# A mixture layer and a diffusion step on one core: where token splits, sums, a weight load and the last rows are placed

## The chip, the cores and the metric

The kernel runs on one core of a Trainium2 chip. TensorE (PE in the profile) multiplies matrices, VectorE (DVE), ScalarE (ACT) and GpSimd (POOL) work elementwise, and SyncE (SP) issues most of the transfers between the chip's memory and the on-chip buffers. Matmul results land in PSUM banks; everything else lies in SBUF. Each engine works through its own instructions in order and waits, where needed, for others. The metric is the device time of one execution in microseconds, the median of several runs. A profiled execution is one more run, and its span is the time from its first to its last instruction.

## The reference

There are 128 batch entries with 64 steps of 256 features each. The first layer is a mixture of experts, the second a step of diffusion over steps and features.

```python
s0 = relu(x @ swi[0]) @ swo[0]               # two shared experts, 256 -> 1024 -> 256
s1 = relu(x @ swi[1]) @ swo[1]
eo = relu(x @ wi[type]) @ wo[type]           # one of five experts by the entry's type
w  = softmax(relu(concat(eo[:,0], s0[:,0], s1[:,0]) @ g1) @ g2)   # from step 0 alone
x  = x + eo*w[0] + s0*w[1] + s1*w[2]
# second layer: edges are reflected, in features (x) and in steps (y)
x  = x + zX*lap_x(x) + zY*lap_y(x) + zR*x*(1 - x)
```

`zX`, `zY` and `zR` are given for each batch entry. All values are 32-bit floats.

## The kernel before, in words

**Precision.** TensorE takes operands of the type fp32r, which are less exact than fp32. The kernel therefore splits each operand into a high part (a ScalarE copy that rounds, called "hi") and a low part (source less hi, on VectorE or GpSimd, "lo"), and forms hi*hi + hi*lo + lo*hi: three matmuls for one product. `split` (L116) writes both parts.

**Seven products.** The first matmul of each expert, on a 2 x 2 grid of blocks, is done with seven block products in place of eight. This needs sums of blocks: `sum_wi` for the weights (S1 to S4), `sum_x` (L194) for the tokens (T1 to T4; T2 needs T1, T4 needs T2). The tokens B11, B21, B22 and T1 to T4 are then split by `split_x` (L207). `unit` (L627) does the seven products: pa with B11 and then B21, pb with T2, T3 and T4 on top of a copy of pa, pd with T1 and then B22. It makes from them four hidden blocks, the h rows of the profile, with the help of u and c. The first two units of the kernel are formed without this scheme (`plain_units`, L676).

**Items.** An item is one expert on two token tiles (of four steps each) and has four units (q = 0 to 3), one for each quarter of the 1024 hidden values. The second matmul (the acc rows) follows one unit behind, in rows i = 0 to 3 of 128 tokens for each of the two tiles: "wide" matmuls over 512 columns take the hi part of the hidden values with both parts of the weights, "narrow" ones over 256 columns take the lo part. `tile_a` and `tile_b` (L738 on) list them, `evacuate` (L747) takes a finished row out of PSUM. The order of the items:

- items 0 and 1: the shared experts on the first two tiles; their rows are kept in memory (sh_d);
- items 100 to 104 (`EI` and on): a typed expert on sixteen batch entries each, gathered by type (`load_fours`, L403), rows stored to memory (eo_d); some 42 us each, from 90 to 304 us;
- groups (`stream`): the typed experts for the batch entries that are left, to 448 us. `store_group` (L920) stores each group's rows. Behind it stand two regions under a condition on the number of slots (`tc.If`, L1100), for batch entries that may not fit; every engine passes their branches;
- items 2 to 15: the shared experts on the other tiles, an even and an odd item for each pair of tiles, some 41.5 us each. Their evacuation adds the row, weighted by the gate, into yb on VectorE. The gate is computed in item 2 (`gate_shared` to `gate_weights`; gis, pt_s and pgs in the profile); diffusion of a finished tile (`diffuse_a` and `diffuse_b`, in two halves; la, lb, lq in the profile) runs in the items behind.

**Order.** Nothing is left to a scheduler in these items: instructions stay on each engine in the order in which the code issues them. Side work is hung at slots k of the item: `at(k, ...)` is the hook behind step k % 4 of unit k // 4, slots 16 and 17 come at the item's end, among the matmuls of its last rows, and slot 17 is behind the last row matmuls that are ahead of the next item. So slots 15 to 17 hold what the next item needs: for expert items `next_fours` places four sums and seven splits of its tokens, for the odd shared items `next_x` (L1117). In `stream` and in the If regions the order is left to the scheduler. SP issues loads and stores in the code's order, and one that waits holds those behind it; the store of the last group goes over GpSimd's queue instead.

**The end.** The last item's last unit is `end_unit` (L824). It forms its hidden values without the seven products, finishes the rows of the first of its two tiles and then those of the second, does diffusion of the last rows between them on VectorE, and takes the last but one step's diffusion on TensorE: fp32 matmuls with diagonal matrices (`diagonals`, the diag and lin rows). The very last step has a neighbour on one side only and goes over VectorE (end_a, end_q).

Every matmul has L88 in the profile (`mm`), every operation of VectorE, ScalarE and GpSimd L103 (`keep`), most loads and stores L114 (`dma`), every branch L1101.

Of the kernel before, what the change touches and what calls it, by code (L numbers as in the profile page):

```python
# [16 lines left out]
P = 128  # L17
# [14 lines left out]
ST = 4  # L32
# [13 lines left out]
def cond_resid_kernel(ctx: ExitStack, tc: tile.TileContext, xg, xs, xn, itok, z, we, ws, g1, g2, out):  # L46
# [356 lines left out]
    def load_fours(n):  # L403

        s0 = (n - EI) * 4 * NB
        gval[n] = expert_of(s0)
        xr = [opool.tile([P, ST + 2, D], F32, tag="yb", name=f"xr{n}_{l}") for l in range(2)]
        xr = [t.rearrange("p r d -> p (r d)")[:, 0 : 4 * S * NB].rearrange("p (j c) -> p j c", c=2 * S) for t in xr]
        load_batches(s0, 4 * NB, lambda j: xr[j // (2 * NB)][:, j % (2 * NB), :])
        for k in range(2):  # L410
            for l in range(2):
                xraw[n, k, l] = xr[l][:, :, k * S : (k + 1) * S]
# [263 lines left out]
    def plain_units():  # L676
# [17 lines left out]
        for i in (T1, T2):  # L694
            sum_x(0, i, vec)
        run(tile(0, 1))
        split_wo(0)
        keep_wo(0)
        sum_wi(2, gps)
# [117 lines left out]
    def diagonals():  # L817

        d = slot2("diag")
        last_op["d"] = [d[:, i * P : (i + 1) * P] for i in range(3)]  # L820
        for dst, f in zip(last_op["d"], (zt[:, 0:1], zt[:, 1:2], cz[:, 0:1])):
            act.activation(dst, ident, AF.Copy, scale=f)

    def end_unit(n, gaps, hooks):  # L824
# [10 lines left out]
        wide, narrow = tile_a(n, q)  # L835
        run(wide)
        run(narrow)
        diffuse_a(t - 1, 0, vec, act)
        run(plain_tile(n, q, 1, w, (last_op["x"], xop[p, B22]), psum, True))
        for i in range(2):  # L840
            run(row_work(n, 1, i, range(NF - 2), True))
        for step in range(3):
            diffuse_b(t - 1, 0, step)
        diffuse_a(t - 1, 1, vec, act)
        halo(t)
        for i in range(2):
            run(row_work(n, 1, i, (NF - 2, NF - 1), True))
            run(row_work(n, 1, i, range(NF), False))
            if i == 0:
                for step in range(3):  # L850
                    diffuse_b(t - 1, 1, step)
        diffuse_a(t, 0, vec, act)
        for step in range(3):
            diffuse_b(t, 0, step)
        for i in range(2, ST):
            if i == ST - 1:
                diffuse_a(t, 1, vec, act)
                for step in range(3):
                    diffuse_b(t, 1, step)
            run(row_work(n, 1, i, range(NF), True))  # L860
            run(row_work(n, 1, i, range(NF), False))

        r = ST
        dx, dy, dc = last_op["d"]
        lin = psum("lin")[:, 0:D]
        mm(lin, dc, y[:, r, :], True, False)
        mm(lin[:, 1:D], dx, y[:, r, 0 : D - 1], False, False)
        mm(lin[:, 0 : D - 1], dx, y[:, r, 1:D], False, False)
        mm(lin[:, 0 : D : D - 1], dx, y[:, r, 1 : D - 1 : D - 3], False, False)
        mm(lin, dy, y[:, r - 1, :], False, False)  # L870
        mm(lin, dy, y[:, r + 1, :], False, True)
        sq, a, q = (small.tile([P, D], F32, tag="s2", name=f"end_{k}") for k in "saq")
        c = y[:, r + 1, :]
        vec.tensor_tensor(a[:, 1 : D - 1], c[:, 0 : D - 2], c[:, 2:D], ALU.add)
        act.activation(q, c, AF.Identity, bias=cz[:, 0:1], scale=cz[:, 1:2])
        edges(a, c, act)
        vec.tensor_mul(q, q, c)
        vec.scalar_tensor_tensor(q, a, zt[:, 0:1], q, ALU.mult, ALU.add)
        vec.scalar_tensor_tensor(q, y[:, r, :], cz[:, 2:3], q, ALU.mult, ALU.add)
        nc.scalar.dma_start(out[:, S - 1, :], q)  # L880
        vec.scalar_tensor_tensor(sq, y[:, r, :], cz[:, 1:2], y[:, r, :], ALU.mult, ALU.mult)
        vec.tensor_tensor(sq, lin, sq, ALU.add)
        nc.sync.dma_start(out[:, S - 2, :], sq)
# [36 lines left out]
    def store_group(g, i):  # L920
        acc = gacc[g][i]
        o = small.tile([P, D], F32, tag="s2", name=f"ge{g}_{i}")
        if g < NRUN - 1:
            act.activation(o, acc[:, 0, :], AF.Copy)
            vec.tensor_add(o, acc[:, 1, :], o)
        else:
            both = small.tile([P, 2, D], F32, tag="s2", name=f"gb{g}_{i}")
            act.activation(both, acc, AF.Copy)
            gps.tensor_add(o, both[:, 0, :], both[:, 1, :])
# [84 lines left out]
    def load_unit(u):  # L1014
        if u < 2 * NQ:
            load_ws(u)
        else:
            load_we(*divmod(u, NQ))
# [42 lines left out]
    def next_fours(n, sums, splits):  # L1061
# [15 lines left out]
        next_fours(EI, (8, 10, 14, 15), (15, 16, 16, 16, 17, 17, 17)),  # L1077
# [4 lines left out]
    for n in range(EI, EI + NQUAD):  # L1082
        parts = [weights_of(n)]
        if n + 1 < EI + NQUAD:
            parts += [
                at(0, lambda: load_fours(n + 1)),
                next_fours(n + 1, (6, 10, 14, 15), (15, 16, 16, 16, 17, 17, 17)),
# [29 lines left out]
    def next_x(p):  # L1117
        if p == NP:
            return {}
        s = {i: [lambda i=i: sum_x(p, i, gps)] for i in (T1, T2, T3, T4)}  # L1120
        x = {i: [lambda i=i: split_x(p, i, gps if i in (B11, B21, B22) else vec)] for i in range(7)}
        return {
            (1, 0): [lambda: load_x(p)],
            (2, 0): s[T1] + s[T2],
            (2, 1): s[T3],
            (2, 2): s[T4] + x[B11],
            (2, 3): x[T2] + x[B21],
            (3, 0): x[T3],
            (3, 1): x[T1],
            (3, 2): x[T4],  # L1130
            (3, 3): x[B22],
        }
# [27 lines left out]
    for p in range(1, NP):  # L1160
        ta, tb = 2 * p, 2 * p + 1
        for e in range(2):
# [19 lines left out]
            elif n == 3:  # L1182
# [3 lines left out]
                parts.append(diffusion(0, 7, True, 7, (0, 1, 1)))  # L1186
# [65 lines left out]
```

## Time and profile before

| | us |
|---|---|
| runs | 1051.44, 1051.68 (median), 1052.11 |
| profiled execution | 1050.79 |
| its span | 1049.1 |
| TensorE busy | 1036.2 |
| VectorE busy | 803.1 |
| ScalarE busy | 570.5 |
| GpSimd busy | 199.5 |

The granted TensorE clock was 0.998 of full speed on the mean. In the timeline a row gives the start, the duration, the engine, the line, the operation, the output and input tiles (without their numbers) and sizes, how many of the same kind follow one another ("x3"), and in square brackets the idle time just before it with what ended it. PEld is TensorE's loading of weights, beside the matmuls. The end of a matmul is modelled, so starts are surer than durations. An engine's name with a q is its own issue of instructions, of a transfer or a branch.

### The profile page before, as it was taken

What the parts mean: (1) busy time and instruction counts of PE and PEld (TensorE: products, weight loads), DVE (VectorE), ACT (ScalarE), POOL (GpSimd) and SP (SyncE); (2) the same over time, 40 slices, a digit from 0 to 9 for tenths busy, and PEclk for the clock granted to TensorE, in tenths of its full rate; (3) what the DMA queues carried; (4) which work ended last, traced back from release to release, by engine and by line L of the source; (5) the groups of instructions that cost most, each with busy time, mean ns of one, the idle gap of its engine ahead of it and who ended that gap; (6) DMA issues with size and microseconds to landing.
All of it is one profiled execution on the core that took longest, in us unless ns stands there. A gap on an engine that the chain in (4) does not pass through costs nothing.

```text
span 1049.1 us, 15713 instructions
## 1 busy us (share of the span) xinstructions
PE 1036.2 (99%) x5433; PEld 882.3 (84%) x5433; DVE 803.1 (77%) x1462; ACT 570.5 (54%) x1081; POOL 199.5 (19%) x199
## 2 busy tenths in 40 slices
PE   9999999999999999999999999999999999999997
PEld 6878888888888889978788888888888888888887
DVE  7887987978777657747979768768687687687777
ACT  6566666766655546643644645446345354364362
POOL 2000000000013001221422521322242242052020
PEclk9999999999999999999999999999999999999999
DMA  6486232331456956555435325334344253254321
GB/s 216 184 286 205 82 103 91 101 121 51 131 178 227 334 175 209 184 180 218 155 127 176 135 107 201 121 121 166 110 166 163 68 209 128 76 175 160 108 76 46
DMA packets 67282, 159.14 MB, mean 152 GB/s; under 512 B 7712, under 2 KB 34848, under 8 KB 67200
## 3 DMA queue, kind: packets, MB, share of 16 engines
q1 hardware_dynamic: 64576, 149.19, 41.1%
q0 software_dynamic: 2480, 8.78, 2.3%
q8 instruction: 44, 0.72, 0.3%
q14 instruction: 38, 0.31, 0.1%
q10 hardware_dynamic: 144, 0.13, 0.0%
HBM read 126.88 MB, written 31.20 MB: 151 GB/s over the span
## 4 chain that ended last, share of the span: by engine, by line
PE 51%; DVE 4%; issue 1%; ACT 1%; DVEq 0%; ACTq 0%
PE acc L88 27%; PE pb L88 10%; PE pd L88 7%; PE pa L88 6%; DVE lq L103 2%; PE pu L88 1%; DVE h_5b L103 0%; DVE pd L103 0%; DVE c L103 0%; PE pgs L88 0%; DVE h_5a L103 0%; ACT u L103 0%; DVE yb L103 0%; DVE la L103 0%; DVE end_q L103 0%
## 5 line engine op out<-in xcount | busy, mean ns | idle before, releaser
L88 PE MATMUL pb<-x,wi 128*128 128x512 f32 x729 | 209.1, 395 | 1.5 <-ACT u L103 1.1
L88 PEld LDWEIGHTS pb<-x,wi 128*128 128x128 f32 x729 | 129.5, 189 | 29.9 <-ACT u L103 5.2
L103 ACT ACTIVATE u<-pb 128x512 f32<-128x512 f32 x162 | 96.8, 597 | 104.3 <-PE pb L88 98.2
L88 PE MATMUL pd<-x,wi 128*128 128x512 f32 x486 | 138.2, 393 | 2.0 <-DVE c L103 1.5
L88 PE MATMUL pa<-x,wi 128*128 128x512 f32 x486 | 137.1, 390 | 0.7 <-PEq L1101 0.7
L103 ACT ACTIVATE pb<-pa 128x512 f32<-128x512 f32 x81 | 47.2, 583 | 129.9 <-PE pa L88 129.9
L103 DVE SCALAR_TENSOR_TENSOR yb<-acc,wgt,yb 128x256 f32<-128x256 f32 x216 | 99.4, 482 | 22.8 <-PE acc L88 19.1
L88 PEld LDWEIGHTS pd<-x,wi 128*128 128x128 f32 x486 | 90.7, 188 | 24.6 <-DVE c L103 4.0
L88 PEld LDWEIGHTS pa<-x,wi 128*128 128x128 f32 x486 | 89.9, 188 | 18.9 <-issue 0.9
L103 DVE TENSOR_TENSOR c<-pd,u 128x512 f32<-128x512 f32 x81 | 55.8, 689 | 38.6 <-ACT u L103 18.6
L103 POOL TENSOR_TENSOR la<-yb 128x508 f32<-128x508 f32 (+1 forms) x28 | 31.7, 1132 | 281.6 <-ACT yb L103 280.0
L103 POOL TENSOR_TENSOR x<-xr,x 128x512 fp32r<-128x512 f32 x23 | 30.8, 1341 | 237.4 <-ACT x L103 156.2
L88 PE MATMUL up<-gxh,gw 128*128 128x256 f32 (+1 forms) x288 | 74.0, 331 | 0.0
L88 PE MATMUL gacc<-gw,gh 128*128 128x512 f32 (+1 forms) x288 | 62.7, 360 | 0.0
L103 ACT ACTIVATE gh<-up 128x256 fp32r<-128x256 f32 (+1 forms) x72 | 34.2, 477 | 42.4 <-PE up L88 41.4
L88 PEld LDWEIGHTS gacc<-gw,gh 128*128 128x128 f32 x288 | 49.9, 188 | 8.4
L88 PE MATMUL acc<-wo,h_1b 128*128 128x256 f32 (+1 forms) x172 | 56.7, 333 | 0.0
L88 PE MATMUL acc<-wo,h_6b 128*128 128x256 f32 (+1 forms) x172 | 56.7, 334 | 0.0
L88 PE MATMUL acc<-wo,h_7b 128*128 128x256 f32 (+1 forms) x172 | 56.7, 333 | 0.0
L88 PE MATMUL acc<-wo,h_2b 128*128 128x256 f32 (+1 forms) x172 | 56.6, 333 | 0.0
L88 PE MATMUL acc<-wo,h_0b 128*128 128x256 f32 (+1 forms) x172 | 56.6, 333 | 0.0
L88 PE MATMUL acc<-wo,h_3b 128*128 128x256 f32 (+1 forms) x172 | 56.6, 333 | 0.0
(253 smaller groups left out, 2536.6 us busy)
## 6 DMA issues: line engine op xcount, KB each, us to landing
wi<-wi_d SPq DMA_DIRECT2D x55, 896.0 KB, 4.5
gwr<-we_in SPq DMA_DIRECT2D x32, 512.0 KB, 5.3
wsr<-we_in SPq DMA_DIRECT2D x20, 512.0 KB, 5.5
xr<-xs_in SPq DMA_DIRECT2D x32, 256.0 KB, 5.6
yb<-xn_in SPq DMA_DIRECT2D x16, 512.0 KB, 5.8
y_out<-lq SPq DMA_DIRECT2D x30, 256.0 KB, 2.1
wi_d<-wi SPq DMA_DIRECT2D x8, 896.0 KB, 4.1
xr<-xg_in SPq DMA_DIRECT2D x80, 64.0 KB, 1.9
```

Source lines behind the costliest of these rows:

```text
L88: nc.tensor.matmul(out_ap, lhsT=lhsT, rhs=rhs, start=start, stop=stop, skip_group_check=True)
L103: ins = call(*args, **kwargs)
```

## The change

- `plain_units`: the split of the first output weights (`split_wo(0)`, with its store) goes ahead of two token sums, T1 and T2, on VectorE.
- `load_fours`: for the first expert item the first weights are asked for ahead of the sixteen gathered loads of tokens; `load_unit` leaves them out later.
- Sums and splits: the first expert item's first two sums move from slots 8 and 10 to 10 and 12. For all expert items the split of T1 moves from slot 17 to 16.
- `store_group`: the last group is evacuated like the others, a ScalarE copy of one half and a VectorE add, in place of a copy of both halves and a GpSimd add.
- `next_x`: for the tokens of items 6 and on, sums go from GpSimd to VectorE at slots 10, 12, 14 and 15, and splits go to slots 15 to 17, with GpSimd left with that of B22 alone. For those of item 4 (made in item 3) GpSimd keeps them, with the splits placed later.
- `diffusion` in item 3: its second half comes three slots sooner.
- `end_unit`: the rows of the first tile are done one by one; diffusion goes ahead of the last hidden values; the last step goes over TensorE as well, with a diagonal of 2 zY, and so the matrices are those of zX, zY and 2 zY.

```diff
@@ load_fours
+        if n == EI:
+            load_we(n, 0)
@@ plain_units
-        for i in (T1, T2):
-            sum_x(0, i, vec)
         run(tile(0, 1))
         split_wo(0)
         keep_wo(0)
+        for i in (T1, T2):
+            sum_x(0, i, vec)
@@ diagonals
-        for dst, f in zip(last_op["d"], (zt[:, 0:1], zt[:, 1:2], cz[:, 0:1])):
+        for dst, f in zip(last_op["d"], (zt[:, 0:1], zt[:, 1:2], cz[:, 2:3])):
@@ end_unit
-        wide, narrow = tile_a(n, q)
-        run(wide)
-        run(narrow)
+        for i in range(ST):
+            for wide in (True, False):
+                run(row_work(n, 0, i, (2 * q, 2 * q + 1), wide))
         diffuse_a(t - 1, 0, vec, act)
-        run(plain_tile(n, q, 1, w, (last_op["x"], xop[p, B22]), psum, True))
+        out_b = plain_tile(n, q, 1, w, (last_op["x"], xop[p, B22]), psum, True)
+        for step in range(3):
+            diffuse_b(t - 1, 0, step)
+        run(out_b)
         for i in range(2):
             run(row_work(n, 1, i, range(NF - 2), True))
-        for step in range(3):
-            diffuse_b(t - 1, 0, step)
         diffuse_a(t - 1, 1, vec, act)
         halo(t)
+        for step in range(3):
+            diffuse_b(t - 1, 1, step)
...
-        mm(lin, dc, y[:, r, :], True, False)
-        mm(lin[:, 1:D], dx, y[:, r, 0 : D - 1], False, False)
-        mm(lin[:, 0 : D - 1], dx, y[:, r, 1:D], False, False)
-        mm(lin[:, 0 : D : D - 1], dx, y[:, r, 1 : D - 1 : D - 3], False, False)
-        mm(lin, dy, y[:, r - 1, :], False, False)
-        mm(lin, dy, y[:, r + 1, :], False, True)
...
+        def beside(dst, row, stop=False):
+            mm(dst[:, 1:D], dx, row[:, 0 : D - 1], False, False)
+            mm(dst[:, 0 : D - 1], dx, row[:, 1:D], False, False)
+            mm(dst[:, 0 : D : D - 1], dx, row[:, 1 : D - 1 : D - 3], False, stop)
+
+        act.activation(qb, b, AF.Identity, bias=cz[:, 0:1], scale=cz[:, 1:2])
+        diffuse_a(t, 1, vec, act)
+        vec.tensor_mul(qb, qb, b)
+        run(row_work(n, 1, 3, range(NF), True))
+        run(row_work(n, 1, 3, range(NF), False))
+        mm(lb, dy, y[:, ST - 1, :], True, False)
+        mm(lc, dyy, b, True, False)
+        beside(lc, c, True)
+        beside(lb, b)
+        mm(lb, dy, c, False, True)
+        act.activation(qc, c, AF.Identity, bias=cz[:, 0:1], scale=cz[:, 1:2])
+        for step in range(2):
+            diffuse_b(t, 1, step)
+        vec.tensor_mul(qc, qc, c)
+        diffuse_b(t, 1, 2)
+        vec.tensor_tensor(qc, lc, qc, ALU.add)
+        nc.scalar.dma_start(out[:, S - 1, :], qc)
+        vec.tensor_tensor(qb, lb, qb, ALU.add)
+        nc.sync.dma_start(out[:, S - 2, :], qb)
@@ store_group
-        if g < NRUN - 1:
-            act.activation(o, acc[:, 0, :], AF.Copy)
-            vec.tensor_add(o, acc[:, 1, :], o)
-        else:
-            both = small.tile([P, 2, D], F32, tag="s2", name=f"gb{g}_{i}")
-            act.activation(both, acc, AF.Copy)
-            gps.tensor_add(o, both[:, 0, :], both[:, 1, :])
+        act.activation(o, acc[:, 0, :], AF.Copy)
+        vec.tensor_add(o, acc[:, 1, :], o)
@@ load_unit
+        if u in wsr:
+            return
@@ items 1 and 100 to 104
-        next_fours(EI, (8, 10, 14, 15), (15, 16, 16, 16, 17, 17, 17)),
+        next_fours(EI, (10, 12, 14, 15), (15, 16, 16, 16, 16, 17, 17)),
...
-                next_fours(n + 1, (6, 10, 14, 15), (15, 16, 16, 16, 17, 17, 17)),
+                next_fours(n + 1, (6, 10, 14, 15), (15, 16, 16, 16, 16, 17, 17)),
@@ next_x
-        s = {i: [lambda i=i: sum_x(p, i, gps)] for i in (T1, T2, T3, T4)}
-        x = {i: [lambda i=i: split_x(p, i, gps if i in (B11, B21, B22) else vec)] for i in range(7)}
...
+        if p == 2:
+            sums, splits, eng, slow = (8, 9, 10, 11), (12, 15, 14, 16, 16, 17, 16), gps, (B11, B21, B22)
+        else:
+            sums, splits, eng, slow = (10, 12, 14, 15), (15, 16, 16, 16, 16, 17, 17), vec, (B22,)
+        return join(
+            at(4, lambda: load_x(p)),
+            *(at(k, lambda i=i: sum_x(p, i, eng)) for i, k in zip((T1, T2, T3, T4), sums)),
+            *(
+                at(k, lambda i=i: split_x(p, i, gps if i in slow else vec))
+                for i, k in zip((B11, T2, B21, T3, T1, T4, B22), splits)
+            ),
+        )
@@ item 3
-                parts.append(diffusion(0, 7, True, 7, (0, 1, 1)))
+                parts.append(diffusion(0, 7, True, 4))
```

## The prediction

> **What bounds the kernel now.** I read the page's engine row first, then the waits of TensorE, then TensorE's timeline around each wait.
>
> ```profile
> PE 1036.2 (99%) x5433; PEld 882.3 (84%) x5433; DVE 803.1 (77%) x1462; ACT 570.5 (54%) x1081; POOL 199.5 (19%) x199
> ```
>
> TensorE is busy for nearly the whole span, VectorE for three quarters, GpSimd for a fifth. So only two things shorten the run: a wait of TensorE, and the stretch behind its last matmul. The waits of TensorE (what it waited for: total us, times, longest):
>
> ```profile
> PE pd L88 <- DVE c L103: 1.5, 1, 1.5
> PE pb L88 <- ACT u L103: 1.1, 4, 0.5
> PE pgs L88 <- DVE gis L103: 1.0, 1, 1.0
> ```
>
> These understate a stall, since the end of a matmul is modelled. In the timeline, 512-column matmuls start every 0.228 us when nothing is late (256-column ones every 0.118), and after a stall the next one takes 0.11 more. So I measure each stall as the distance of two starts less that rate, and add 0.11. An expert boundary shows it:
>
> ```profile
> 132.19 0.39 PE L88 MATMUL acc<-wo,h_7b 128*128 128x512 f32 x1
> 132.64 0.73 PE L88 MATMUL pb<-x,wi 128*128 128x512 f32 x2
> ```
>
> 0.45 between two starts, less 0.228, plus 0.11: 0.33 us, with no wait shown at all. Everything below is in these units. The span is 1049.1 us, its execution 1050.79, the runs' median 1051.68: the median lies 0.9 above the profiled execution, and I carry that over.
>
> **The change part by part.**
>
> *Start (plain units).* TensorE's first row matmul comes at 14.06 instead of 13.42 (0.65 with the 0.11), waiting for the VectorE split wo of 13.32 to 14.00. VectorE had made two sums at 10.80 and 11.52 before it. With the sums behind it, wo is done at about 13.3, before TensorE asks at 13.5. But the two sums (0.60 + 0.72) then push later VectorE work; a gap of 0.42 at 21.3 takes part of it, and c of the first full unit, at about 26.2, would meet a TensorE that arrives 0.65 sooner, at 25.95. That gives back 0.4. Value 0.25; ends 0 and 0.65.
>
> *First expert weights and sums (load_fours, slots 10 and 12).* The dearest stall, on VectorE and then on TensorE:
>
> ```profile
> 68.05 0.69 DVE L103 TENSOR_TENSOR xt<-xr,xr 128x512 f32<-128x512 f32 x1 [2.48 <-DMA xr<-xg_in]
> ...
> 69.26 0.68 DVE L103 TENSOR_TENSOR wi<-wsum,wi 128x512 fp32r<-128x512 f32 x1
> 69.86 0.69 DVE L103 TENSOR_TENSOR c<-pd,u 128x512 f32<-128x512 f32 x1
> ...
> 70.60 0.98 PE L88 MATMUL pd<-x,wi 128*128 128x512 f32 x3 [1.50 <-DVE c L103]
> ```
>
> The sum waits 2.48 us for the gathered tokens, and c, for which TensorE waits, stands behind it. TensorE's start at 68.24 needed three matmuls (0.69), so 68.93 against 70.60: 1.66 + 0.11 = 1.77. Two slots later the sum is behind c; c's inputs are there at about 67. The weights, too, came late: SP asks for 16 token rows first, then for the weights.
>
> ```profile
> 56.65 9.60 SPq L114 DMA_DIRECT2D xr<-xg_in  x16
> 68.05 0.34 SPq L114 DMA_DIRECT2D wsr<-we_in  x1
> 75.67 0.98 PE L88 MATMUL pb<-x,wi 128*128 128x512 f32 x3 [0.20 <-ACT u L103]
> ```
>
> They landed at 74.41; ScalarE's split of them stood in front of u, and TensorE stalled 0.36 + 0.11. Asked for ahead of the rows they land near 62. The price: SP issues a table read and that transfer first, about 0.75 us, so the last token row lands near 68.8 instead of 68.03. Behind the waiting sum on VectorE now stand h_5b, h_5a and the pd add of that unit; their first reader on TensorE is the narrow rows at about 75, so some 5 us of cover hide it. SP's stores behind the rows move by 0.75, then regain it, as the later weight load is gone from there. Value 2.2; ends 1.8 and 2.3.
>
> *T1's split from slot 17 to 16.* At each of five expert boundaries (90, 132, 174, 216, 258 us) pb, a ScalarE copy, waits behind three copies of x, which wait behind the second eo copy:
>
> ```profile
> 130.44 1.14 ACT L103 ACTIVATE x<-xt 128x512 fp32r<-128x512 f32 x2
> ...
> 132.00 0.59 ACT L103 ACTIVATE pb<-pa 128x512 f32<-128x512 f32 x1
> ```
>
> One of the three, 0.52 us, moves ahead of the eo copies, where ScalarE waits on TensorE anyway; each stall is 0.2 without its 0.11. All five go: 0.27 + 4 x 0.325 = 1.57. Value 1.55; ends 1.2 and 1.6.
>
> *Last group's add.* GpSimd leaves it, so gis no longer waits for GpSimd's branches:
>
> ```profile
> 448.78 0.73 POOL L103 TENSOR_TENSOR ge<-gb 128x256 f32<-128x256 f32 x1 [9.07 <-ACT gb L103]
> 452.53 0.69 DVE L103 COPY gis<-pt_s 128x512 f32<-128x512 f32 x1 [6.15 <-POOLq L1101]
> 453.27 2.05 PE L88 MATMUL pgs<-gis,g1t 128*128 128x128 f32 x16 [0.98 <-DVE gis L103]
> ```
>
> That stall is 1.15. But VectorE itself now adds first and then passes the two branches, and the next item's pa waits for VectorE to be past them. Half copies (0.38, as an eo copy) end near 448.5 and 448.75, the adds (0.41) at 448.9 and 449.3; VectorE's table read and two branches took 1.18 before (445.97 to 447.15). That gives 450.1 to 450.5 for pa, which started at 449.03: a new wait of 1.1 in place of 1.15. Behind VectorE there stands only gis. The store of the group comes some 0.6 sooner, which nobody waits for. Value 0; ends -0.4 and +0.5.
>
> *Item 3 (diffusion earlier, sums off GpSimd's way).* Stalls at 520.48 (0.70 + 0.11), 521.97 (0.41 + 0.11) and three small ones: 1.65. They come where diffusion's second half meets GpSimd's sums. Three slots (2.5 us each) earlier that half is out of the way, but must fit among the gate's row additions. Value 1.0; ends 0.4 and 1.65.
>
> *Items 5 to 13, odd ones: four sums and two splits from GpSimd to VectorE.* This is the part to weigh. While GpSimd works, VectorE is slow:
>
> ```profile
> 601.26 1.66 DVE L103 SCALAR_TENSOR_TENSOR h_5b<-c,h_5b 128x512 fp32r<-128x512 f32 x1 [0.70 <-ACT h_5b L103]
> 602.84 0.68 DVE L103 SCALAR_TENSOR_TENSOR h_5a<-pb,h_5a 128x512 fp32r<-128x512 f32 x1
> ```
>
> h_5b takes 1.66, its twin 0.68. In item 5 four such rows are longer by 0.57, 0.43, 0.44 and 0.97: 2.4 us lost to GpSimd. The Trainium skill (SBUF — State Buffer, "Who interferes with whom") says that VectorE with two SBUF inputs and GpSimd share one port pair as an exclusive lock, and that the second to issue fully blocks. By the rule the six operations, 1.30 each, may cost VectorE 7.8, and taking them over (6 x 0.60 = 3.6) would free 4.2 us; by the row they cost 2.4, and VectorE has 1.2 us more to do per odd item. I take the row: VectorE goes from 32.87 busy in 42 us to about 34.1. Stalls to be won: item 5 0.45, 7 0.44, 11 0.52, 13 0.28: 1.67.
>
> Against that, VectorE's order at the end of the item. With t = 0 at the next item's first matmul, TensorE wants T2 after pa (0.7) and eight wide rows (1.8), at 2.5; B21 at 3.2, T3 at 5.7, T1 at 6.4, T4 at 9.0, B22 at 9.7. The item's first four rows end by t = -4.2 (ten wide and sixteen narrow matmuls follow: 2.3 + 1.9); their eight evacuations of 0.48, the first at -4.8 as row 0 ends sooner, keep VectorE until about -1.1; then T2 at -0.5, B21 0.1, T3 0.7, T1 1.3; four more evacuations to 3.2, T4 3.8. Smallest slack 3.0 us. ScalarE has no evacuations here, so pb isn't late. I leave 0.1 per boundary for what I can't see: value 1.2; ends -1.5 (a 0.6 us stall at each of five) and +1.7.
>
> *Tail.* The last row's matmuls end here, and everything behind is exposed:
>
> ```profile
> 1042.36 0.48 DVE L103 SCALAR_TENSOR_TENSOR yb<-acc,wgt,yb 128x256 f32<-128x256 f32 x1
> 1042.89 0.70 PE L88 MATMUL lin<-yb,diag 128*128 128x256 f32 x2 [0.29 <-DVE yb L103]
> 1045.53 0.42 DVE L103 TENSOR_TENSOR end_s<-lin,end_s 128x256 f32<-128x256 f32 x1
> 1045.99 0.33 SPq L883 DMA_DIRECT2D y_out<-end_s  x1
> ```
>
> The row's last matmul starts at 1039.96, but VectorE, continuous since 1025.66, takes its result only at 1042.36. Diffusion now goes ahead of the hidden layer's last part and the rows of the first tile end one by one, so VectorE catches up and reads the row at about 1040.3, done 1040.8. Then nine fp32 matmuls in place of six, two passes of 0.215 each: those that need the last row (three for lc, four for lb) run 1041.2 to 1044.1. Of the VectorE chain behind the row (six operations, 3.1 us) only two adds are left: qb at 1044.5, the store at 1044.55 against 1045.99. Value 1.4; ends 0.9 (VectorE not caught up) and 2.0.
>
> Sum: 0.25 + 2.2 + 1.55 + 0 + 1.0 + 1.2 + 1.4 = 7.6. Profiled execution 1050.8 - 7.6 = 1043.2; median 1051.7 - 7.6 = 1044.1. All ends together: -0.4 + 0 + 1.8 + 1.2 + 0.4 - 1.5 + 0.9 = 2.4 and 10.4 (1049.3 and 1041.3).
>
> **The rivals.**
>
> *The last group's new wait is longer than the old.* VectorE's branches are passed after the adds, and both TensorE's pa and the gate hang on it. For: 1.18 us is measured with VectorE already waiting there. Against: ScalarE and TensorE passed theirs meanwhile, so only VectorE's own path counts. With 1.5 us more than I put: 1045.6, between 1045 and 1047.
>
> *VectorE gives back what GpSimd frees.* Splits move from slots 10 to 15 into 15 to 17, all in the stretch where it also evacuates. At 0.6 us per odd boundary: 1.2 + 1.5 = 2.7 less gain, 1046.8 (1046 to 1049). For: 1.2 us more work; B22, still on GpSimd, can hold the lock against an evacuation. Against: 3 us of slack, and that expert items already work in this order with only ScalarE's stall.
>
> *Slower.* The same place with a large price: VectorE reaches T2 over 3.0 us after my placement, and every us beyond it stalls TensorE at each of five boundaries. It decides at a lateness of 3.0 + (7.6 - 1.2 + 2.1) / 5 = 4.7 us: then 1054. That takes five of the eight evacuations at the contended 1.66 - 0.68 = 1 us more, with a single GpSimd split there to contend with.
>
> *The tail and item 3 give all.* 2.0 + 1.65 and the start's 0.65: 1.7 more, 1042.4; with the last group's 0.5, 1041.9.
>
> **How the numbers follow.** Likeliest (each part within its ends, 1042 to 1046): 0.62. Longer branch wait 0.12, VectorE gives back 0.15, more than my sum (below 1042) 0.05, slower 0.04, no difference 0.02. A measurement of this kernel tells 0.2%, 2.1 us, from nothing. Faster: 0.62 + 0.12 + 0.15 + 0.05 = 0.94. Predicted 1044.1; the range 1041.8 to 1047.3 leaves out the slow half of the give-back, the two last cases and what is below 1041.8.
>
> **What would show it.** Starts of TensorE: no gap at 13.4, 68.9 and 75.3; no gap at the five boundaries; a wait before item 2's first matmul of 2 us in place of 0.9, and none before pgs; h_5b in odd items at 0.7; the last yb row done before 1041 less the 6 us gained ahead. I am wrong if gaps of 0.3 or more stand at the boundaries behind items 5, 7, 9, 11 and 13, if VectorE is still continuous at the last row, or if pa of item 2 starts over 3 us after the group's last matmul.

## The result, and the profile after

Six runs of each kernel: before, 1052.11 us in the median (1051.44 to 1053.70); changed, 1043.73 us (1042.41 to 1046.41). The ratio is 0.9919, with a 95% interval of 0.9903 to 0.9935: 8.4 us less. Forecast was 1044.1, a gain of 7.6. The profiled execution of the changed kernel took 1042.87 us, with a span of 1040.7.

The page's engine row of the changed kernel, and under it the waits of TensorE (what it waited for: total us, times, longest):

```profile
PE 1031.7 (99%) x5439; PEld 884.7 (85%) x5439; DVE 810.3 (78%) x1492; ACT 572.5 (55%) x1081; POOL 154.4 (15%) x167
...
PE pa L88 <- DVEq L1104: 1.7, 1, 1.7
...
PE pb L88 <- ACT pb L103: 0.5, 2, 0.3
PE pd L88 <- DVE c L103: 0.4, 1, 0.4
```

GpSimd lost 45 us of work and VectorE gained 7. Of the three waits of before that hung on c, u and gis, two are gone from the list and one is small; a new one stands at the top, pa waiting for VectorE's sequencer.

The 8.4 us by stretches of TensorE's timeline, each from one fixed matmul to another, so that every stall in between is counted, shown or not:

| stretch | before | after | gain | forecast |
|---|---|---|---|---|
| span's start to the wide rows behind pm_cnt (start) | 39.32 | 39.40 | -0.1 | 0.25 |
| from there to the middle of item 100 (first expert weights and sums, first boundary) | 63.29 | 61.27 | 2.0 | 2.5 |
| to the middle of item 104 (four boundaries) | 167.79 | 166.25 | 1.5 | 1.25 |
| to the last group's last matmul | 177.62 | 177.61 | 0 | 0 |
| to a matmul in item 2's first unit (last group's add) | 8.30 | 8.10 | 0.2 | 0 |
| to a matmul ahead of item 3's stalls | 54.63 | 54.61 | 0 | 0 |
| to pd in item 4 (items 3 and 4) | 48.38 | 47.24 | 1.1 | 1.0 |
| to the last row's last matmul (items 5 to 15) | 480.63 | 478.53 | 2.1 | 1.2 |
| from there to the span's end (tail) | 9.13 | 7.65 | 1.5 | 1.4 |

The forecast column splits T1's 1.55 into 0.3 for the first boundary and 1.25 for the others. It adds up to 7.6; the gains add up to 8.4, the difference of the spans.

Where the sum waited for tokens before, the changed kernel has c ahead of it (SyncE's loads of the token rows, then VectorE's and ScalarE's timeline):

```profile
57.65 10.23 SPq L114 DMA_DIRECT2D xr<-xg_in  x16
...
67.64 0.69 DVE L103 TENSOR_TENSOR c<-pd,u 128x512 f32<-128x512 f32 x1 [0.19 <-PE pd L88]
68.24 0.68 DVE L103 TENSOR_TENSOR wo<-wsr,wo 128x512 fp32r<-128x512 f32 x1
69.68 0.69 DVE L103 TENSOR_TENSOR xt<-xr,xr 128x512 f32<-128x512 f32 x1 [0.75 <-DMA xr<-xg_in]
...
71.49 0.69 DVE L103 TENSOR_TENSOR pd<-pd,u 128x512 f32<-128x512 f32 x1
...
72.21 0.60 ACT L103 ACTIVATE h_4b<-pd 128x512 fp32r<-128x512 f32 x1 [1.04 <-DVE pd L103]
72.70 0.61 ACT L103 ACTIVATE wi<-wsr 128x256 fp32r<-128x256 f32 x2
73.21 0.59 ACT L103 ACTIVATE u<-pb 128x512 f32<-128x512 f32 x1
```

The stall of 1.77 is gone. But the sum still waits, now for 0.75, as the last token row landed at 69.60, and this wait reaches TensorE: the pd add (the row pd<-pd,u) stands behind the sum, ScalarE's h_4b waits for the pd add, and u, for which TensorE waits, stands behind h_4b and the weights' split (wi). TensorE's matmuls start at 73.33 and 73.86, 0.52 apart where 0.23 is due: with the 0.11 behind it 0.40 is left, where 0.47 stood before.

An expert boundary, TensorE's timeline at the place of the one shown of before:

```profile
130.25 0.39 PE L88 MATMUL acc<-wo,h_7b 128*128 128x512 f32 x1
130.47 0.84 PE L88 MATMUL pb<-x,wi 128*128 128x512 f32 x3
```

0.22 between the starts in place of 0.45. The last group (TensorE, VectorE):

```profile
445.03 0.76 DVE L103 TENSOR_TENSOR ge<-gacc,ge 128x256 f32<-128x256 f32 x2 [2.14 <-ACT ge L103]
...
446.55 0.98 PE L88 MATMUL pa<-x,wi 128*128 128x512 f32 x3 [1.74 <-DVEq L1104]
...
448.07 0.69 DVE L103 COPY gis<-pt_s 128x512 f32<-128x512 f32 x1 [2.28 <-PE pt_s L490]
...
449.69 1.95 PE L88 MATMUL pgs<-gis,g1t 128*128 128x128 f32 x16
```

pa starts 2.02 us after the group's last matmul (1.01 before), and pgs starts without a wait. The tail:

```profile
1033.01 0.28 PE L88 MATMUL acc<-wo,h_7b 128*128 128x256 f32 x1
...
1033.33 0.48 DVE L103 SCALAR_TENSOR_TENSOR yb<-acc,wgt,yb 128x256 f32<-128x256 f32 x1
...
1036.80 0.42 DVE L103 TENSOR_TENSOR end_qb<-lin_b,end_qb 128x256 f32<-128x256 f32 x1 [0.99 <-PE lin_b L88]
...
1037.25 0.33 SPq L889 DMA_DIRECT2D y_out<-end_qb  x1
```

VectorE takes the last row 0.32 us after its last matmul starts (2.40 before). From yb's start to the store it is 3.92 us (3.63 before), most of it now TensorE's work.

### The profile page after: what moved, and what is told of

Same layout as the page of the kernel before. It is cut to its first block, busy times and chain, and to the rows that moved or that the text cites. A ratio compares the mean times of both kernels' runs of the same rounds, so it can differ in the third digit from the quotient of the medians.

```text
span 1040.7 us, 15721 instructions
## 1 busy us (share of the span) xinstructions
PE 1031.7 (99%) x5439; PEld 884.7 (85%) x5439; DVE 810.3 (78%) x1492; ACT 572.5 (55%) x1081; POOL 154.4 (15%) x167
## 4 chain that ended last, share of the span: by engine, by line
PE 56%; DVE 1%; issue 0%; ACT 0%; DVEq 0%; ACTq 0%
PE acc L88 30%; PE pb L88 11%; PE pa L88 7%; PE pd L88 7%; PE pu L88 1%; DVE lq L103 0%; PE lin_b L88 0%; PE pgs L88 0%; PE lin_c L88 0%; PE pge L88 0%; DVE h_3a L103 0%; DVE c L103 0%; ACT u L103 0%; DVE pd L103 0%; DVE h_2b L103 0%
## 5 line engine op out<-in xcount | busy, mean ns | idle before, releaser
L88 PE MATMUL acc<-wo,h_4b 128*128 128x256 f32 (+1 forms) x172 | 56.5, 332 | 0.0
```

What stands on the lines that cost most here:

```text
L88: nc.tensor.matmul(out_ap, lhsT=lhsT, rhs=rhs, start=start, stop=stop, skip_group_check=True)
```

## The experiments

All kernels below are the changed one with the edit shown. Executions of one kernel lie up to 5 us apart (1042.41 to 1046.41 of the changed one, 1044.52 to 1049.60 of the first one below). Profiles of the same code differ in the first 10 us, in the two stalls at 73 and 82 us, in one stall of item 4 and, as will be seen, behind the last group. So the stretches of the profile decide, each read from a single profile, and the medians are given beside them.

### First expert weights: behind the token rows again

```diff
-        if n == EI:
-            load_we(n, 0)
```

> The changed kernel, with the first expert weights asked for where they were before, behind the sixteen token rows; the sums stay at their new slots. Of the two stalls near 70 us the first (1.77) should stay away, as it hung on the sum's slot alone. The second was 0.47 before and is still 0.40 in the changed kernel, where the weights are early: there ScalarE's h_4b waits for VectorE's pd add, which stands behind the sum that waits for tokens. If the weights' landing was a second cause behind it, the stall grows to 1 us or more here, since the split of the weights waits for them at about 74.5 while TensorE asks at 73.5. If h_4b alone makes it, it stays at 0.4 or, with the tokens 0.75 us earlier, goes to nothing.

1045.72 us in the median. The first stall stayed away; the second grew from 0.40 to 1.74. ScalarE's and TensorE's timeline:

```profile
74.50 0.61 ACT L103 ACTIVATE wi<-wsr 128x256 fp32r<-128x256 f32 x2 [2.07 <-DMA wsr<-we_in]
75.02 0.58 ACT L103 ACTIVATE u<-pb 128x512 f32<-128x512 f32 x1
...
75.65 0.73 PE L88 MATMUL pb<-x,wi 128*128 128x512 f32 x2 [1.47 <-ACT u L103]
```

So the early weights are needed. Moving the sum alone removes 1.77 at the first place and, since TensorE then arrives sooner, has 1.3 of it fall due at the second, where the weights are late. No run moved the weights alone; that c would then still wait behind the sum is argued from the profile before. From pm_cnt to the first group's first matmul the kernel takes 1.85 us more than the changed one.

### T1's split at slot 17 again

```diff
-(15, 16, 16, 16, 16, 17, 17)
+(15, 16, 16, 16, 17, 17, 17)      # in both calls of next_fours
```

> The changed kernel, with the split of T1 of the expert items back at slot 17. My theory: each of the five boundaries gets its stall of 0.27 to 0.33 us back, 1.5 us in all in the profile, and nothing else moves. Rival: the boundaries gained for another reason (GpSimd, or work that is earlier for the edits ahead of them), and stay without a stall.

One execution, 1044.76 us. All five stalls came back, 0.27 at the first boundary and 0.32 to 0.33 at the others. TensorE's timeline at the second:

```profile
131.14 0.39 PE L88 MATMUL acc<-wo,h_7b 128*128 128x512 f32 x1
131.59 0.73 PE L88 MATMUL pb<-x,wi 128*128 128x512 f32 x2
```

0.45 again. The sum of the five is 1.55. The stretch that holds the last four grew by 1.47, a little more than their starts show (1.28).

### Items 5 to 13: the engine and the place apart

The edit moves work to VectorE and moves it later. Two kernels undo one of the two.

```diff
 # the old engine at the new slots
-(10, 12, 14, 15), (15, 16, 16, 16, 16, 17, 17), vec, (B22,)
+(10, 12, 14, 15), (15, 16, 16, 16, 16, 17, 17), gps, (B11, B21, B22)
```

> The changed kernel, with the four sums and the splits of B11 and B21 of items 6 and on given back to GpSimd, at the new, late slots. If the work on VectorE is what removed the stalls of items 5, 7, 11 and 13 (GpSimd slowing VectorE), they come back in other places of the odd items, with VectorE rows of 1.0 to 1.8 us beside GpSimd's: 1.5 to 3 us over the changed kernel. If it is the later placement alone, no stall over 0.2 us stands in items 5 to 13 and the time is that of the changed kernel within 0.5 us.

```diff
 # the new engine at the old slots
-(10, 12, 14, 15), (15, 16, 16, 16, 16, 17, 17), vec, (B22,)
+(8, 8, 9, 10), (10, 11, 11, 12, 13, 14, 15), vec, (B22,)
```

> The changed kernel, with the sums and splits of items 6 and on kept on VectorE but at the slots of before (8 to 15). If GpSimd's slowing of VectorE made the stalls, they stay away: the changed kernel's time within 0.5 us. If the placement matters, VectorE's added 3.6 us now stand in the middle of the item, among c and the hidden blocks and beside the diffusion of the tile before, and the stalls of ScalarE's u and VectorE's c return at 0.3 us or more in each odd item: 1.5 to 2.5 us longer.

Medians: 1046.00 and 1046.69 us. From the gate's last matmuls in item 2 to the last row's last matmul, which holds items 3 to 15:

| | slots of before | new slots |
|---|---|---|
| GpSimd | 2.1 longer | 565.73: 2.3 longer |
| VectorE | 567.27: 3.8 longer | 563.43 |

The times are in us, and "longer" is against the changed kernel, lower right. The upper left figure is worked out from the kernel before, less the 1.1 that items 3 and 4 gained. Neither half of the edit gains anything alone; one costs a little, the other 1.7. VectorE's timeline in item 5, first of the kernel with GpSimd at the new slots:

```profile
592.77 1.19 DVE L103 SCALAR_TENSOR_TENSOR lq<-la,zt,lq 128x512 f32<-128x512 f32 x1
593.88 0.68 DVE L103 SCALAR_TENSOR_TENSOR h_4a<-pa,h_4a 128x512 fp32r<-128x512 f32 x1
594.49 1.45 DVE L103 SCALAR_TENSOR_TENSOR lq<-lb,zt,lq 128x512 f32<-128x512 f32 x1
595.86 0.68 DVE L103 TENSOR_TENSOR c<-pd,u 128x512 f32<-128x512 f32 x1
```

The diffusion rows lq take 1.19 and 1.45 while GpSimd makes its sums, and c, behind them, holds TensorE for 0.56 + 0.11, here and in two of the other four odd items. Then of the kernel with VectorE at the old slots:

```profile
596.57 0.68 DVE L103 TENSOR_TENSOR xt<-xr,xr 128x512 f32<-128x512 f32 x1
597.17 0.69 DVE L103 TENSOR_TENSOR c<-pd,u 128x512 f32<-128x512 f32 x1
597.77 0.68 DVE L103 TENSOR_TENSOR xt<-xr,xt 128x512 f32<-128x512 f32 x1
598.37 0.68 DVE L103 TENSOR_TENSOR x<-xr,x 128x512 fp32r<-128x512 f32 x1
```

Every row has its 0.68, but three sums stand ahead of c and two more rows right behind: c waits for its turn, 0.44 + 0.11 at TensorE, and once more 0.11, in each of the five odd items. In the changed kernel:

```profile
593.70 0.74 DVE L103 SCALAR_TENSOR_TENSOR lq<-lb,zt,lq 128x512 f32<-128x512 f32 x1
594.57 0.69 DVE L103 TENSOR_TENSOR c<-pd,u 128x512 f32<-128x512 f32 x1
595.18 0.68 DVE L103 TENSOR_TENSOR xt<-xr,xr 128x512 f32<-128x512 f32 x1
```

Short rows, and the sum behind c. The expectation for the first kernel was right in kind; that for the second, that a free port alone keeps the stalls away, fell.

### Item 3: diffusion's second half late again

```diff
-parts.append(diffusion(0, 7, True, 4))
+parts.append(diffusion(0, 7, True, 7, (0, 1, 1)))
```

> The changed kernel, with the second half of the diffusion in item 3 back at its old slots (seven later); the new slots of GpSimd's sums and splits in item 3 stay. The changed kernel lost 0.4 us to stalls in item 3, the one before 1.7. If diffusion's place is what mattered, a stall of u or h_4b near 518 us comes back with 0.7 to 1.3 us. If GpSimd's sums, which now start one slot apart, mattered, item 3 stays within 0.2 us of the changed kernel.

1043.17 us. The stall of u came back:

```profile
517.01 0.39 PE L88 MATMUL acc<-wo,h_5a 128*128 128x512 f32 x1
517.92 0.96 PE L88 MATMUL pb<-x,wi 128*128 128x512 f32 x3 [0.53 <-ACT u L103]
```

0.91 apart: 0.69 + 0.11. Up to item 4's stall the kernel is 0.67 longer. Items 3 to 15 are only 0.38 longer, though: item 4's stall of c, 0.65 in the changed kernel, is 0.30 here. It looks as if item 4 gave back what item 3 gains, but that isn't shown: of the nine other profiles with the changed code in items 3 and 4, five have 0.65 there and four 0.37 or 0.38, and what makes the difference is open. Item 3 itself was 1.43 longer before the change, so diffusion's place is worth about half of that. For the other 0.76 GpSimd's new slots in item 3 are left, which no run tried alone.

### Start: the two sums ahead again

```diff
+        for i in (T1, T2):
+            sum_x(0, i, vec)
         run(tile(0, 1))
         split_wo(0)
         keep_wo(0)
-        for i in (T1, T2):
-            sum_x(0, i, vec)
```

> The changed kernel, with the two token sums back ahead of the split of the first output weights. In the changed kernel the wait for wo is gone, but pb of the first full unit waits 0.5 us for the bank that VectorE's h_2b frees, behind the same two sums; from the first row matmul's place to the pm_cnt matmul both kernels take the same time. My theory: VectorE sets the pace in the first 21 us, and the order of its work only moves the wait; the wait for wo returns with 0.65, that of pb goes, and the time is that of the changed kernel within 0.3 us. Rival: the edit gained its 0.25 us and hid it behind a later landing of the first loads; then this kernel shows the wait for wo and a wait of pb, and is longer by 0.25 to 0.65.

1042.97 us. The wait for wo came back (0.55) and that of pb at 21 us (0.52) went. From the last matmul ahead of the wait for wo to pm_cnt it takes 25.55 us here, 25.60 in the changed kernel and 25.66 before. The edit moved the wait, and no gain shows: in eight other profiles that start like the changed kernel this stretch takes 25.17 to 25.82.

### Tail: the last step on VectorE again

```diff
-        lb, lc = (psum(f"lin_{k}")[:, 0:D] for k in "bc")
...
-        vec.tensor_tensor(qc, lc, qc, ALU.add)
...
+        vec.scalar_tensor_tensor(q, a, zt[:, 0:1], q, ALU.mult, ALU.add)
+        vec.scalar_tensor_tensor(q, y[:, r, :], cz[:, 2:3], q, ALU.mult, ALU.add)
```

> The changed kernel, with the very last step back on VectorE (as before the change, six fp32 matmuls with a diagonal of cz), while the order ahead of it (rows one by one, diffusion sooner) stays. In the changed kernel 7.7 us lie between the start of the last row matmul and the end of the span, in the one before 9.1. My theory: most of the 1.45 us gained comes from the order, since VectorE takes the last row 0.3 us after its last matmul and not 2.4; the matrices for the last step only move work from VectorE (3.6 us from the row to the store before) to TensorE (3.9 us). But with three more diffusion operations back ahead of the row (1.3 us) VectorE is about 1 us late for it. So 8.2 to 8.8 us here, 0.5 to 1.1 more than the changed kernel. Rival: the order alone gains all, and this kernel ends in 7.7 us or less; or it gains nothing, and the distance is 9.1 again.

1043.86 us. The tail takes 8.44 us: 0.8 more than in the changed kernel, 0.7 less than before. (In the other profiles with the changed tail it takes 7.34 to 7.80.) VectorE's timeline:

```profile
1034.06 0.48 DVE L103 SCALAR_TENSOR_TENSOR lq<-lb,zt,lq 128x256 f32<-128x256 f32 x1
1034.46 0.48 DVE L103 SCALAR_TENSOR_TENSOR yb<-acc,wgt,yb 128x256 f32<-128x256 f32 x1
1034.97 0.42 DVE L103 TENSOR_TENSOR end_a<-yb 128x254 f32<-128x254 f32 x1
...
1037.64 0.42 DVE L103 TENSOR_TENSOR end_s<-lin,end_s 128x256 f32<-128x256 f32 x1
```

The row is taken 1.4 us after its last matmul starts (1033.06), between 0.32 and 2.40. The new order and the new place of the last step gain about half each. The second gains not by a shorter way from row to store, but by the three lq rows that no longer have to come ahead of the row.

### Last group: who frees what

Three kernels. The first, with ScalarE copying both halves and VectorE adding from SBUF:

```diff
-        act.activation(o, acc[:, 0, :], AF.Copy)
-        vec.tensor_add(o, acc[:, 1, :], o)
+        act.activation(both, acc, AF.Copy)
+        vec.tensor_add(o, both[:, 0, :], both[:, 1, :])      # last group alone
```

> The changed kernel, with one thing altered: the last group's accumulators are copied out whole by ScalarE (both halves, as before the change), and VectorE adds the two halves from SBUF. My theory: item 2's first matmul waited 1.9 us in the changed kernel because the PSUM bank that it takes is freed by VectorE's add, behind which lie VectorE's branches. With ScalarE freeing the bank, the distance from the group's last matmul to pa falls from 2.02 to about 1.0 us, gis still doesn't wait for GpSimd, and pgs follows without a stall: 1.0 us less than the changed kernel, about 1042.7. Rival: TensorE waits for VectorE's branch for the sake of the order of the regions, not of the bank; then pa stays at 2.0 us and nothing changes.

1045.53 us. TensorE's timeline:

```profile
449.26 0.50 PE L88 MATMUL pa<-x,wi 128*128 128x512 f32 x1 [2.17 <-DVEq L1109]
```

pa came 2.45 us after the group's last matmul, not 1.0: the bank isn't what it waits for. VectorE's adds came later by the longer copies, and its branches with them. pa starts 0.29 us behind the start of VectorE's second branch in both kernels (446.26 and 446.55 in the changed one, 448.97 and 449.26 here). My theory fell, and the rival held in kind.

The second is the kernel with four edits, of which the first bears on this place:

```diff
+                    for k in range(2):      # last group: both halves into one
+                        mm(gacc[g][i][:, 0, :], h[j][0][:, i * P : (i + 1) * P], w[j][:, k, 256:512], ...)
...
-        vec.tensor_add(o, acc[:, 1, :], o)
...
-next_fours(EI, (10, 12, 14, 15)
+next_fours(EI, (11, 12, 14, 15)
...
-        for i in (T3, T4):
-            sum_x(0, i, vec)
         run(tile(1, 1, seeded))
+        for i in (T3, T4):
+            sum_x(0, i, vec)
...
-diffusion(2, 6)
+diffusion(2, 7)
```

> The changed kernel with four small edits, each at its own place. (1) Last group: TensorE adds both halves itself (two matmuls of 256 columns into one half in place of one of 512), so that ScalarE's copy is all that is left and neither VectorE nor GpSimd has an add; pa should come 1.0 us after the group's last matmul in place of 2.0, with no wait ahead of pgs and no stretch at half clock behind it. (2) First expert's T1 sum at slot 11 in place of 10, behind the pd add: h_4b isn't held any more, and the stalls at 73.3 (0.40) and 82 (0.38) should go. (3) The sums T3 and T4 of the first tile behind the hidden block h_3b: pb's bank is free 1.4 us sooner, and its stall of 0.5 goes. (4) Item 4's diffusion of tile 2 one slot later: c is no longer behind three long rows, and the stall of 0.65 at 554 goes. Together 1.0 + 0.7 + 0.5 + 0.6 = 2.8 us less than the changed kernel. If TensorE waits for something else at any of the places, that term is missing.

1045.91 us; none of the four terms gained. (1) VectorE passed its branches ahead of time, yet pa waited 1.89 us for TensorE's own (PEq): its second branch took 1.38 us in place of the 0.22 that it takes in every other profile here. The trace doesn't tell why. (2) The stall at 73 went, but the one at 82 grew from 0.38 to 1.01: VectorE waited 0.59 for the next weights, and T4's sum and B11's split stood ahead of h_6b. (3) pb's stall grew from 0.52 to 1.01: its bank was free, but ScalarE's copy of T3, ahead of pb, now waited 1.47 for the sum. (4) In item 4 two stalls of 0.3 stand in place of one of 0.65.

The third gives the add back to GpSimd, and gis a buffer that GpSimd hasn't used:

```diff
+            act.activation(both, acc, AF.Copy)
+            gps.tensor_add(o, both[:, 0, :], both[:, 1, :])
...
-        g = gate_in["s"] = small.tile([P, 4, P], F32, tag="s2", name="gis")
+        g = gate_in["s"] = slot4("gis", F32)[:, 0, :].rearrange("p (i c) -> p i c", i=4)
```

> The changed kernel, with the last group's halves added by GpSimd as before the change, and gis put into a buffer that GpSimd doesn't use. VectorE then has nothing behind the group's last matmul and passes its branches early. My theory: item 2's first matmul waits for VectorE's passing of the branches, wherever its last work ends, and gis waited for GpSimd only for the buffer's sake. So pa comes 1.0 us after the group's last matmul (2.0 in the changed kernel), pgs follows without the stall of 1.3 that it had before: 1.0 us less than the changed kernel in the profile. And since a stall of 2.0 us or more was followed in two of the profiles by some 3.5 us of matmuls at half clock, and one of 1.0 us never was, no half clock shows here. Rival: TensorE's own branches take as long (1.4 us for one of them in the kernel with four edits), then pa comes 2 us after it here too.

1041.45 us (1040.84 to 1041.84), ratio to before 0.9902 (0.9886 to 0.9919). TensorE's and VectorE's timeline:

```profile
446.15 0.94 PE L88 MATMUL pa<-x,wi 128*128 128x512 f32 x3 [0.79 <-PEq L1109]
...
449.25 0.94 PE L88 MATMUL pgs<-gis,g1t 128*128 128x128 f32 x7
...
447.90 0.69 DVE L103 COPY gis<-pt_s 128x512 f32<-128x512 f32 x1 [4.46 <-PE pt_s L490]
```

pa comes 1.07 us after the group's last matmul and pgs in its turn. From there to the gate's last matmuls it takes 24.12 us, against 25.05 in the changed kernel and 25.27 before. Both waits were avoidable: that for GpSimd by another buffer, that for VectorE by giving it nothing to do there. All four executions lie below all six of the changed kernel, but the two were measured at different times, and the intervals of their ratios to before overlap.

### A faster version

The last kernel, and two edits to order:

```diff
+        run(tile(1, 1, seeded))
         for i in (T3, T4):
             sum_x(0, i, vec)
-        run(tile(1, 1, seeded))
-        split_x(0, T3, vec)        # now at slot 8 of item 0
...
-next_fours(EI, (10, 12, 14, 15), (15, 16, 16, 16, 16, 17, 17))
+next_fours(EI, (11, 12, 14, 16), (16, 16, 16, 16, 16, 17, 17))
```

> The kernel with GpSimd's add and gis in a buffer of its own, and two more edits. Start: the sums T3 and T4 come behind h_3b and the split of T3 goes to slot 8, so that neither VectorE's sums nor ScalarE's copy stand ahead of pb. First expert item: T1's sum at slot 11, T4's sum and B11's split at 16, so that neither pd add nor h_6b stands behind them. If TensorE's small stalls near 21 us (0.5) and at 73 and 82 us (0.8 together) hang on the order alone, they go: 1.3 us less than without them, 2.3 less than the changed kernel. If VectorE is simply full in the first 85 us, they come back a little later with most of that: then within 0.5 us of the kernel without the two edits.

1040.40 us (1040.11 to 1042.82), ratio to before 0.9900 (0.9883 to 0.9916); span 1038.6, against 1039.7 of the kernel that it is built on and 1040.7 of the changed one. The stalls at 73 and 82 are gone (0.99 in the kernel that it is built on), with this at the place of u:

```profile
73.63 0.39 PE L88 MATMUL acc<-wo,h_5a 128*128 128x512 f32 x1
73.86 0.84 PE L88 MATMUL pb<-x,wi 128*128 128x512 f32 x3
```

The start's stall only moved, from 21 to 23 us (0.52). So near 80 us the order was the cause: in the nine profiles with the changed order there, the two stalls come to 0.6 to 1.1 together. In the first 25 us three orders of VectorE's work left a stall of half a us somewhere, though not in every execution: one profile of the changed order has none at 21 us.

## Why the prediction was right, and where it wasn't

**The total.** 7.6 forecast, 8.4 measured, the median 0.4 below the predicted time. T1's split, the tail and the first of the two stalls near 70 us went as worked out, the odd items in kind, and item 3 in part; for the start no gain shows. That the total came so near is in part luck: the first experts and the start fell short by 0.5 and 0.3, and the odd items gave 0.9 more.

**First experts: two steps failed**, the price and the cover. I had the last token row land 0.75 us later, near 68.8; then the sum would hardly have waited, as VectorE is ready for it only at about 68.9. It landed at 69.60, 1.57 later: SyncE began with the rows 1.00 later and took 10.23 us to issue them in place of 9.60. And I wrote that the "first reader on TensorE is the narrow rows at about 75", so that 5 us hide the wait. The pd add's first reader is ScalarE's h_4b, and u, on which TensorE hangs sooner, stands behind that in ScalarE's order. The cover can be read off nine profiles with this code here. The sum's wait differs from 0.47 to 0.95, and less TensorE's stall at u (without the 0.11) it leaves 0.45 or 0.46 in every one of them; with a wait of 0.47 or 0.48 there is no stall at u. So the cover is 0.46 us, not 5. Behind it the stall at h_6b differs too, so that the two stalls, 0.65 together before, come to 0.6 to 1.1. In the changed kernel's profile 0.40 stayed at u and 0.2 was added at h_6b. Hence 1.7 in place of 2.2 without the boundary. That the weights had to come sooner as well was right.

**Last group.** A new wait of 1.1 in place of the old 1.15: measured 2.02 less 1.01, and -1.3 at pgs. I took the first for the price of the edit; it was avoidable. What I left out altogether is the clock. A stall of 2 us stands where one of 1 us stood, and in two of the profiles with such a stall TensorE ran at half clock behind it. The windows of the kernel with VectorE at the old slots (us, then the busy time of PE, PEld, DVE, ACT and POOL, then granted clock, DMA share, GB/s):

```profile
445.00:447.00 2.00, 0.26 (x3) 0.13 (x2) 0.76 (x2) 0.59 (x2) 0.60 (x1) 1.00 0.00 0
447.00:449.00 2.00, 2.00 (x8) 1.52 (x9) 0.26 (x1) 0.58 (x1) 0.54 (x1) 0.70 0.34 121
449.00:451.00 2.00, 2.00 (x6) 1.52 (x6) 0.43 (x1) 0.60 (x1) 0.38 (x1) 0.50 0.07 23
451.00:453.00 2.00, 2.00 (x19) 1.92 (x17) 0.69 (x1) 0.60 (x1) 1.65 (x2) 0.95 0.23 66
```

From the group's last matmul to the gate's last it takes 26.27 us there, 25.05 in the changed kernel's profile with the very same code at this place: 1.2 us, in some executions and not in others. The Trainium skill (TensorE: Matmul & The Clock Gate, the part on the clock gate) has the clock fall to half after an idle window of about 3.4 us and counts windows that run freely; here two starts 2.02 and 2.45 us apart were enough once each, and in eight other profiles 2.0 to 2.2 us weren't. By the page's figure this stall would be too short, so the measurement decides; but its warning against idle gaps bears on the edit, and I hadn't weighed it. Where the stall falls doesn't decide it either. The starts of a profile's clock records lie whole multiples of 3.41 us apart; on that grid the stall lay whole in one stretch in both profiles with half clock, but also in four of the eight without. Nor can half clock there be the whole reason why the kernel with GpSimd's add is 2.3 us faster in the median where the profiles differ by 1.0. Such a stretch lowers an execution's mean clock by 0.0016, and of the three executions of the changed kernel above 1044 us two have 1.000. That stays open.

**Odd items: the term was mis-sized.** 1.2 forecast, 2.1 measured. The stalls counted one by one gave 1.67, the items' lengths give 2.0: before, items 5, 7, 11 and 13 took 41.94, 41.88, 41.94 and 41.65 us, and in the changed kernel all take 41.35. Item 5's stall stood here before:

```profile
605.25 0.40 PE L88 MATMUL acc<-wo,h_5a 128*128 128x512 f32 x1
605.81 0.96 PE L88 MATMUL pb<-x,wi 128*128 128x512 f32 x3 [0.17 <-ACT u L103]
```

The same two start 0.23 apart in the changed kernel (600.26 and 600.49). No boundary stalled, so the 0.5 that I kept back was for nothing. Over items 5 to 12, one window of the kernel before:

```profile
576.03:908.59 332.56, 332.10 (x1698) 282.99 (x1697) 250.93 (x403) 162.69 (x276) 91.97 (x84) 1.00 0.39 140
```

and one of the changed kernel:

```profile
571.18:901.95 330.77, 330.77 (x1698) 283.49 (x1697) 256.90 (x427) 164.12 (x276) 57.57 (x60) 1.00 0.40 140
```

VectorE (the third busy time) has 24 instructions more and 6.0 us more to do: 1.5 for each of four odd items, where the row gave 1.2 and my sum by the rule a relief of up to 4.2. But it was my sum that was far off, not the rule. GpSimd's operation beside the h_5b of 1.66 us at 601.26:

```profile
601.07 1.30 POOL L103 TENSOR_TENSOR x<-xr,x 128x512 fp32r<-128x512 f32 x1
```

1.11 us of it were left when h_5b began, and h_5b took 0.97 longer than its shortest, 0.68. It is so in every case: in items 5 to 15 of the kernel before, 29 VectorE rows without an operand in PSUM began with over 0.3 us of a GpSimd operation left, and each took longer than the shortest of its kind by that rest less 0.12 to 0.19. The 82 rows with an operand in PSUM that began so lost 0.02 at most. So VectorE, where it is the second to issue, is blocked for nearly the whole rest, as the rule has it. But in item 5 only four rows of VectorE meet GpSimd's six operations in that way, and that is 2.4 us and not 7.8. Nor is h_5a a twin on the port: its input pb lies in PSUM, and it takes 0.68 beside GpSimd too.

What I had put down to the engine, though, needs the place as well, as the two half edits showed.

**Start.** 0.25 forecast, no gain seen. I named the give-back, but at c; it came at pb, which waits for the bank that h_2b frees, behind the same sums.

**T1 and the tail.** 1.55 and 1.4; measured 1.8 (0.3 and 1.5) and 1.5. The starts at the five boundaries alone give 1.57. For the tail the sum held, with TensorE's nine matmuls done 3.4 us after yb starts where the sum had 3.8.

## What to carry to other kernels

To price a wait that is moved, follow the readers of everything behind it on every engine, not only on the one that bounds: the next reader here was a copy on a third engine that stood in front of the one that mattered. When two engines block each other at a port, price the pairs that meet there, not the length of all operations. When work moves to another engine and to another place at once, each half can cost what the whole gains. And what VectorE did last ahead of a branch was waited for by TensorE behind it, even where ScalarE had freed the bank; on GpSimd, with a buffer of its own for gis, the same add cost nothing.

## What the hardware showed that I had not expected

A stall of 2.0 to 2.5 us was followed in two profiles by 3.41 us at half clock (granted 0.50, matmuls 0.43 us apart in place of 0.228), and in eight others not.

The first matmuls, the pm_idle rows from 1.3 us on, were about 0.42 us apart in every profile, six or seven in a row. In several profiles useful matmuls were too, up to eight in a row. The profile has no record of the clock there: its first one, full clock, begins behind them, at 9.68 us in the profile with the eight and at 3.97 in the changed kernel's. (Where there is no record, a window shows 1.00.) In the first of the two the pm_cnt matmul came 2.3 us later than in the other. What sets the time of that first record no run here shows.

One branch of TensorE took 1.38 us in one build and 0.22 in the twelve others. And a row of VectorE without an operand in PSUM lost nearly all that was left of a GpSimd operation under way, less 0.12 to 0.19 us, in each of 29 cases.
